# Bias additions in two halves, an ordered A^T, one warming matmul fewer and outputs sent by ScalarE, in a four-layer graph kernel on one core

## The chip, the cores and the metric

The kernel runs on one core of a Trainium2 chip, in one launch. The metric is the device time in microseconds (us); the median of several runs counts. The engines have short names in the profile: PE is TensorE (PEld its weight loads), DVE is VectorE, ACT is ScalarE, POOL is GpSimd and SP is SyncE, which here only issues DMAs.

## The reference

64 graphs share one adjacency A of 256 nodes, with 128 features for each node. Four layers follow each other; each adds its result to its input and normalises over the features. Cut to what matters:

```python
def reference(x, adj, ...):            # x [64, 256, 128], adj [256, 256], float32
    # layer 0: Chebyshev stack A x, A^2 x, A^3 x, with both adjacencies the same one
    x = layernorm(x + sum_k (A^k x) W_k)
    # layer 1
    x = layernorm(x + A (x W) + bias)
    # layer 2: A_norm = D^-1/2 (A + I) D^-1/2
    x = layernorm(x + (A_norm x) W^T + b)
    # layer 3: five steps of a gated unit, input h = x
    for step in range(5):
        m = A h                         # in_matrix and out_matrix are both A
        av = concat(m, m)
        u3 = h @ u3_w.T + u3_b
        z = sigmoid(av @ w3_w.T + w3_b + u3)
        r = sigmoid(av @ w4_w.T + w4_b + u3)
        hv = tanh(av @ w5_w.T + w5_b + (r * h @ u5_w.T + u5_b))
        h = (1 - z) * h + z * hv
    return layernorm(x + h)
```

## The kernel before

The 64 graphs are cut into 32 groups of two. A group's features fill one tile of 128 partitions by 512 (two graphs, two halves of the nodes, 128 features), and its whole path through the four layers is recorded as a list of operations. A group is named by its first graph: 0, 2, 4 and so on to 62.

The order of the instructions is not written by hand. Every operation is put into a planner with an engine, a cost, a lag until its result counts as there, a rank (mostly the group's number) and its inputs and outputs. `Plan.order` makes twelve attempts at a list schedule. The first has the bare ranks; in the others each rank has a small random addition. The attempt with the shortest planned end gives the order in which all instructions are issued, each engine's queue in that order. Any changed operation can therefore change the order everywhere. The planner's costs and lags are fixed numbers in the code: an SP load of x, for example, has a lag of its own for each of the first four groups, whatever else is on its way. Up to twelve groups are in flight, each some stages behind the one before.

Matrix products with A run in two forms. For the first three groups and at the start they are plain. For the others a product with a 2x2 block matrix is done in seven block products instead of eight (`seven` and `inner_seven`): GpSimd builds differences of the inputs (ts at L806 and L810, tq at L813), TensorE multiplies in an opening, one block more, and the rest; ScalarE saves the first block before it is added to (us, usq, usg at L848) and VectorE puts the blocks together (m, mq, mg at L832 to L842). "pm", "pmq", "pmg" are the PSUM banks of such products. In layer 0 VectorE also forms sums of two SBUF tiles (sd L690, ss L693, se L696, sf L699).

Normalisation in layers 0 to 2 is `spread_of` and `normalise_centred`: ScalarE squares and accumulates (L551), GpSimd takes the power −1/2 (rs, L555), ScalarE scales (L612). In layers 1 and 2 GpSimd adds the bias to the layer's input (yb, L977, in `record`), and VectorE adds this to the product of TensorE (s, L619). For 28 groups the state of layer 3 goes out to DRAM and comes back in another layout (dn, hn) before VectorE adds the residual (s, L624).

At the start, TensorE does seven warming matmuls on zeros. Then it transposes A (`turned_early`, banks p_at0 and p_at1), ScalarE and VectorE copy one half each to aT (`halved`, L298 and L299), TensorE squares A (`square`, p_a), and the two halves of A^2 transposed are copied in the same way. Between these stand the transposes ptx of the first loads of x. float32 matmuls stand in the trace as two passes.

At the end, the last two groups, 60 and 62, use `ended`. Their outputs lie in two PSUM banks of 256 columns; ScalarE squares the first half (L575), VectorE takes the statistics of the second (L580 to L584), GpSimd the power (L595). Then ScalarE scales a quarter (L599), VectorE the other half and after it the quarter that is left (L590), and SP sends the two halves (L604).

The DMAs of the kernel are nearly all issued from SP, in the order of its queue; GpSimd issues eight small loads of biases.

Of the kernel before, what the change touches and what calls it, by code (L numbers as in the profile page):

```python
# [12 lines left out]
OP = mybir.AluOpType  # L13
AX = mybir.AxisListType

P = 128
# [6 lines left out]
FINE = 8  # L23
END = 8
STEPS = 5
WARM = 7
ONES = (0, 0)
EPS = 1e-5
BANKS = 8
# [151 lines left out]
def kernel(  # L181
# [30 lines left out]
    nc = tc.nc  # L212
# [25 lines left out]
    def pre(rank, engine, cost, run, reads=(), writes=(), lag=None, joint=False, after=()):  # L238
        lag = lag or {"SP": 2300, "PE": 260, "DVE": 260, "ACT": 130, "POOL": 100}[engine]
        return plan.add(engine, cost, lag, rank, run, reads, writes, after, joint)  # L240
# [55 lines left out]
    def halved(v, ps):  # L296

        pre(-8, "ACT", act_cost(N), lambda: nc.scalar.copy(v.ap[:, 0, :], ps[0].ap[:, :N]), [ps[0]], [v], joint=True)  # L298
        pre(-8, "DVE", 420, lambda: nc.vector.tensor_copy(v.ap[:, 1, :], ps[1].ap[:, :N]), [ps[1]], [v], joint=True)  # L299

    for mt in range(T):
        pre(-8, "PE", 440, lambda mt=mt: turned_early(mt), [a_nat], [p_at[mt]])
    halved(aT, p_at)
    for mt in range(T):
        pre(-8, "PE", 870, lambda mt=mt: square(mt), [a_nat, aT], [p_a2[mt]])
    halved(a2T, p_a2)


# [162 lines left out]
    class Group:  # L471
# [90 lines left out]
        def ended(self, s):  # L562


            y, st, mv, ve, rs = (self.val(k, n + "3") for k, n in (
                ("w", "y"), ("st", "st"), ("mv", "mv"), ("ve", "ve"), ("rs", "rs")))
            halves = [range(t * self.q // 2, (t + 1) * self.q // 2) for t in range(2)]

            def place(q):
                t, i = divmod(q, self.q // 2)  # L570
                return s[t].ap[:, i * P:(i + 1) * P]

            def squares():
                for q in halves[0]:
                    nc.scalar.activation(nat(y)[:, q, :], place(q), AF.Square, scale=C ** -0.5,  # L575
                                         bias=root[:, 0:1], accum_out=ve.ap[:, q:q + 1])

            def stats():
                for q in halves[1]:
                    nc.vector.bn_stats(st.ap[:, q * 6:(q + 1) * 6], place(q))  # L580
                for q in halves[1]:
                    nc.vector.bn_aggr(mv.ap[:, 2 * q:2 * q + 2], st.ap[:, q * 6:(q + 1) * 6])
                q = halves[1]
                nc.vector.tensor_scalar(ve.ap[:, q.start:q.stop], mv.ap.rearrange("p (q k) -> p k q", k=2)[:, 1, q.start:q.stop],  # L584
                                        EPS, None, op0=OP.add)

            def scaled(t, first):
                q, n = halves[t], self.q // 2
                lo = q.start + first
                nc.vector.tensor_tensor(nat(y)[:, lo:q.stop, :], s[t].ap[:, first * P:n * P].rearrange("p (q c) -> p q c", c=C),  # L590
                                        rs.ap[:, lo:q.stop, None].to_broadcast([P, n - first, C]), op=OP.mult)

            self.act(squares, [s[0]], [y, ve], 390 * self.q // 2, True)
            self.dve(stats, [s[1]], [st, mv, ve], 260 * self.q // 2 + 110, True)
            self.add("POOL", 1040, 100, lambda: nc.gpsimd.tensor_tensor(rs.ap, ve.ap, half[:, :self.q], op=OP.pow),  # L595
                     [ve], [rs])
            h0, h1 = Val("const", [P, 1], "y0"), Val("const", [P, 1], "y1")
            h0.tile = h1.tile = root
            self.act(lambda: nc.scalar.mul(nat(y)[:, 0, :], place(0), rs.ap[:, 0:1]), [s[0], rs, y], [h0], 390)  # L599
            self.dve(lambda: scaled(1, 0), [s[1], rs, y], [h1], 380)  # L600
            self.dve(lambda: scaled(0, 1), [s[0], rs, y, h0], [h0], 230)
            for t, h in ((1, h1), (0, h0)):
                q = halves[t]
                self.add("SP", 450, 2400, lambda q=q: nc.sync.dma_start(self.view(out)[:, q.start:q.stop], nat(y)[:, q.start:q.stop]),  # L604
                         [y, h], [])

        def normalise_centred(self, tag, s):
            y, rs = self.spread_of(tag, s)
# [337 lines left out]
        def record(self):  # L946
# [26 lines left out]
            for tag, ats, w, bias in (("1", aT, w1c, b1c), ("2", anT, w2T, b2c)):  # L973
                yb = self.val("w", "yb" + tag)

                def biased(yb=yb, y=y, bias=bias):
                    nc.gpsimd.tensor_tensor(nat(yb), nat(y), bias[1][:, None, :].to_broadcast([P, self.q, C]),  # L977
                                            op=OP.add)

                self.add("POOL", 40 + 625 * self.nb, 100, biased, [y, bias[0]], [yb])  # L980
                m = self.propagate(tag, y, ats)
                py = self.val("bank", "py" + tag)

                def weight(py=py, m=m, w=w):
                    for q in range(self.q):
                        mm(py.ap[:, q * P:(q + 1) * P], m.ap[:, q * P:(q + 1) * P], w[1], True, True)

                self.pe(pe_cost(P, self.q), weight, [m, w[0]], [py])
                y = self.normalise_centred(tag, self.added(tag, py, yb))
# [107 lines left out]
```

## Time and profile before

| what | value |
|---|---|
| median of 3 runs | 1331.43 us (1331.15 to 1331.56) |
| the profiled execution's own time | 1330.67 us |
| its span in the trace | 1328.9 us, 23277 instructions |
| PE busy | 1319.2 us, 99% |
| DVE, ACT, POOL busy | 1038.5 us, 771.5 us, 630.7 us |
| L977 (bias additions), 64 of 128x512 | 82.8 us, 1294 ns each |
| L806 (differences of 128x256) | 730 to 742 ns each |

Busy times add up what each engine worked on, also where another engine sets the pace, so an engine with a high share is not always the one that is waited for. A line of a group has the line of code, the engine, the operation, output and inputs by name, shapes, a count, then the sum of busy time, the mean length in ns, and the idle time of the engine before it with what ended it. A line of the timeline has the start and the length in us first; neighbouring instructions of one kind are merged (xcount), and their length is that of the whole row. In a list of waits an engine and the tile that it works on stand first, then what it waited for, then the sum in us, how often, and the longest.

### The profile page before, as it was taken

What the parts mean: (1) busy time and instruction counts of PE and PEld (TensorE: products, weight loads), DVE (VectorE), ACT (ScalarE), POOL (GpSimd) and SP (SyncE); (2) the same over time, 40 slices, a digit from 0 to 9 for tenths busy, and PEclk for the clock granted to TensorE, in tenths of its full rate; (3) what the DMA queues carried; (4) which work ended last, traced back from release to release, by engine and by line L of the source; (5) the groups of instructions that cost most, each with busy time, mean ns of one, the idle gap of its engine ahead of it and who ended that gap; (6) DMA issues with size and microseconds to landing.
All of it is one profiled execution on the core that took longest, in us unless ns stands there. A gap on an engine that the chain in (4) does not pass through costs nothing.

```text
span 1328.9 us, 23277 instructions
## 1 busy us (share of the span) xinstructions
PE 1319.2 (99%) x6907; PEld 925.0 (70%) x6907; DVE 1038.5 (78%) x2574; ACT 771.5 (58%) x2360; POOL 630.7 (47%) x994
## 2 busy tenths in 40 slices
PE   9999999999999999999999999999999999999998
PEld 8987656657767866656677777676767876565555
DVE  7967777888797777778878777888877778777786
ACT  4777553545557765545465675655555688444445
POOL 4887531426176464415264573634434575222222
PEclk9999999999999999999999999999999999999999
DMA  7422343635234433545344333433441224444433
GB/s 186 122 59 63 90 107 82 154 95 133 73 87 112 112 88 89 127 108 139 95 115 109 88 96 96 106 93 104 104 104 56 66 63 142 98 108 92 95 80 95
DMA packets 402589, 133.87 MB, mean 101 GB/s; under 512 B 309760, under 2 KB 374400, under 8 KB 402464
## 3 DMA queue, kind: packets, MB, share of 16 engines
q1 hardware_dynamic: 402208, 132.26, 39.5%
q8 instruction: 55, 0.90, 0.3%
q0 software_dynamic: 256, 0.13, 0.2%
q14 instruction: 70, 0.57, 0.1%
HBM read 66.78 MB, written 65.27 MB: 99 GB/s over the span
## 4 chain that ended last, share of the span: by engine, by line
PE 99%; DVE 1%; issue 0%; ACT 0%; POOLq 0%; DVEq 0%; ACTq 0%
PE pr L222 31%; PE ph L222 21%; PE pmg L222 19%; PE py L222 12%; PE pm L222 7%; PE pz L222 4%; PE pmq L222 4%; PE s L222 1%; PE warm L222 0%; PE p_a L222 0%; DVE se L696 0%; DVE s L624 0%; PE ptx L863 0%; DVE sf L699 0%; POOLq L1092 0%
## 5 line engine op out<-in xcount | busy, mean ns | idle before, releaser
L222 PE MATMUL pr<-mg,w435u5T 128*128 128x512 f32 x640 | 321.0, 593 | 1.4 <-DVE mg L842 1.4
L806 POOL TENSOR_TENSOR tsg<-h 128x256 f32<-128x256 f32 x128 | 94.0, 734 | 306.4 <-DMA h<-dh 216.9
L912 ACT ACTIVATE r<-pr,bsum 128x512 f32<-128x512 f32 x160 | 105.5, 659 | 127.5 <-PE pr L222 111.3
L912 ACT ACTIVATE pr<-pr,bsum 128x512 f32<-128x512 f32 x160 | 105.4, 659 | 122.6 <-PE pr L222 122.0
L555 POOL TENSOR_TENSOR rs<-ve,half 128x4 f32<-128x4 f32 x98 | 100.5, 1026 | 147.6 <-ACT y L551 132.1
L943 DVE TENSOR_TENSOR d<-ph,hT 128x512 f32<-128x512 f32 x158 | 108.2, 685 | 71.5 <-ACT ph L912 67.3
L222 PE MATMUL ph<-rh,w435u5T 128*128 128x512 f32 x320 | 163.1, 593 | 0.0
L222 PE MATMUL pr<-hT,w2u3T 128*128 128x512 f32 x320 | 162.8, 593 | 0.0
L222 PE MATMUL ph<-mg,w435u5T 128*128 128x512 f32 x320 | 162.5, 593 | 0.0
L551 ACT ACTIVATE y<-s,root 128x128 f32<-128x128 f32 x392 | 152.8, 393 | 16.1 <-DVE s L619 13.5
L222 PEld LDWEIGHTS pr<-mg,w435u5T 128*128 128x128 f32 x640 | 109.0, 191 | 72.6 <-issue 57.4
L912 ACT ACTIVATE ph<-ph,bsum 128x512 f32<-128x512 f32 x158 | 104.0, 659 | 65.8 <-PE ph L222 65.1
L943 DVE TENSOR_TENSOR rh<-r,hT 128x512 f32<-128x512 f32 x160 | 109.1, 682 | 32.0 <-ACT r L912 30.7
L222 PEld LDWEIGHTS pmg<-aTp,h 128*128 128x128 f32 x512 | 88.0, 190 | 65.6 <-issue 43.0
L612 ACT ACTIVATE y<-s,rs 128x128 f32<-128x128 f32 x384 | 122.1, 393 | 4.5 <-POOL rs L555 4.1
L943 DVE TENSOR_TENSOR pr<-pr,d 128x512 f32<-128x512 f32 x156 | 107.6, 692 | 1.8 <-ACT pr L912 0.5
L943 DVE TENSOR_TENSOR hT<-hT,pr 128x512 f32<-128x512 f32 x156 | 105.7, 679 | 1.9
L222 PE MATMUL pmg<-s_aTp,tsg 128*128 128x128 f32 x768 | 106.7, 275 | 0.0
L222 PEld LDWEIGHTS ph<-rh,w435u5T 128*128 128x128 f32 x320 | 58.5, 190 | 63.5 <-issue 44.8
L977 POOL TENSOR_TENSOR yb<-y,wb 128x512 f32<-128x512 f32 x64 | 82.8, 1294 | 29.0 <-ACT y L612 28.9
L222 PE MATMUL pmg<-aTp,h 128*128 128x128 f32 x512 | 96.3, 274 | 0.0
L222 PEld LDWEIGHTS pmg<-s_aTp,tsg 128*128 128x128 f32 x768 | 96.0, 192 | 0.0
(212 smaller groups left out, 2782.2 us busy)
## 6 DMA issues: line engine op xcount, KB each, us to landing
dh<-th SPq DMA_DIRECT2D x160, 256.0 KB, 2.1
h<-dh SPq DMA_DIRECT2D x512, 64.0 KB, 2.4
x<-in_x_dram SPq DMA_DIRECT2D x32, 256.0 KB, 3.4
hT<-dh SPq DMA_DIRECT2D x128, 64.0 KB, 2.0
out_dram<-y SPq DMA_DIRECT2D x30, 256.0 KB, 2.4
dx<-tx SPq DMA_DIRECT2D x29, 256.0 KB, 2.6
xT<-dx SPq DMA_DIRECT2D x58, 128.0 KB, 2.6
dn<-tn SPq DMA_DIRECT2D x28, 256.0 KB, 2.0
```

Source lines behind the costliest of these rows:

```text
L222: nc.tensor.matmul(o, lhsT, rhs, start=start, stop=stop, skip_group_check=shared)
L551: nc.scalar.activation(nat(y)[:, q, :], nat(s)[:, q, :], AF.Square, scale=C ** -0.5, bias=root[:, 0:1], accum_out=ve.ap[:, q:q + 1])
L555: nc.gpsimd.tensor_tensor(rs.ap, ve.ap, half[:, :self.q], op=OP.pow)
L612: nc.scalar.mul(nat(y)[:, q, :], nat(s)[:, q, :], rs.ap[:, q:q + 1])
L806: nc.gpsimd.tensor_tensor(ts.ap[:, :2 * P].rearrange("p (x c) -> p x c", x=2), ins(h)[:, 1], ins(h)[:, :, 0], op=OP.subtract)
L912: self.act(lambda: nc.scalar.activation(t.ap, ps.ap, func, bias=bias[1], scale=1.0), [ps, bias[0]], [t], act_cost(self.width) + 100)
L943: self.dve(lambda: nc.vector.tensor_tensor(out(t), way(a), way(b), op=op), [a, b], [t])
L977: nc.gpsimd.tensor_tensor(nat(yb), nat(y), bias[1][:, None, :].to_broadcast([P, self.q, C]), op=OP.add)
```

## The change

- `WARM` is 6 instead of 7.
- The transposes and squares of A are chained in the plan, so that half 0 stands before half 1 on TensorE. Before, p_at1 came before p_at0.
- `ended`: ScalarE scales its whole half (`multiplied`), VectorE only the other (`scaled`). ScalarE's queue issues the DMA for its own half, SP's queue the other.
- Each bias addition on GpSimd becomes two instructions on 256 of the 512 columns. They are separate operations for the planner, with a cost of 735 each.

```diff
-WARM = 7
+WARM = 6
...
+    behind = ()
     for mt in range(T):
-        pre(-8, "PE", 440, lambda mt=mt: turned_early(mt), [a_nat], [p_at[mt]])
+        behind = (pre(-8, "PE", 440, lambda mt=mt: turned_early(mt), [a_nat], [p_at[mt]], after=behind),)
     halved(aT, p_at)
     for mt in range(T):
-        pre(-8, "PE", 870, lambda mt=mt: square(mt), [a_nat, aT], [p_a2[mt]])
+        behind = (pre(-8, "PE", 870, lambda mt=mt: square(mt), [a_nat, aT], [p_a2[mt]], after=behind),)
     halved(a2T, p_a2)
...
-            def scaled(t, first):
-                q, n = halves[t], self.q // 2
-                lo = q.start + first
-                nc.vector.tensor_tensor(nat(y)[:, lo:q.stop, :], s[t].ap[:, first * P:n * P].rearrange("p (q c) -> p q c", c=C),
-                                        rs.ap[:, lo:q.stop, None].to_broadcast([P, n - first, C]), op=OP.mult)
+            def multiplied():
+                for q in halves[0]:
+                    nc.scalar.mul(nat(y)[:, q, :], place(q), rs.ap[:, q:q + 1])
+
+            def scaled():
+                q = halves[1]
+                nc.vector.tensor_tensor(nat(y)[:, q.start:q.stop, :], s[1].ap[:, :len(q) * P].rearrange("p (q c) -> p q c", c=C),
+                                        rs.ap[:, q.start:q.stop, None].to_broadcast([P, len(q), C]), op=OP.mult)
...
-            self.act(lambda: nc.scalar.mul(nat(y)[:, 0, :], place(0), rs.ap[:, 0:1]), [s[0], rs, y], [h0], 390)
-            self.dve(lambda: scaled(1, 0), [s[1], rs, y], [h1], 380)
-            self.dve(lambda: scaled(0, 1), [s[0], rs, y, h0], [h0], 230)
-            for t, h in ((1, h1), (0, h0)):
-                q = halves[t]
-                self.add("SP", 450, 2400, lambda q=q: nc.sync.dma_start(self.view(out)[:, q.start:q.stop], nat(y)[:, q.start:q.stop]),
-                         [y, h], [])
+            self.act(multiplied, [s[0], rs, y], [h0], 770)
+            self.dve(scaled, [s[1], rs, y], [h1], 420)
+            for engine, e, q, h in (("SP", nc.sync, halves[1], h1), ("ACT", nc.scalar, halves[0], h0)):
+
+                def sent(e=e, q=q):
+                    e.dma_start(self.view(out)[:, q.start:q.stop], nat(y)[:, q.start:q.stop])
+
+                self.add(engine, 450, 2400, sent, [y, h], [])
...
-                def biased(yb=yb, y=y, bias=bias):
-                    nc.gpsimd.tensor_tensor(nat(yb), nat(y), bias[1][:, None, :].to_broadcast([P, self.q, C]),
-                                            op=OP.add)
-
-                self.add("POOL", 40 + 625 * self.nb, 100, biased, [y, bias[0]], [yb])
+
+                def biased(part, yb=yb, y=y, bias=bias):
+                    nc.gpsimd.tensor_tensor(nat(yb)[:, part], nat(y)[:, part],
+                                            bias[1][:, None, :].to_broadcast([P, self.q // 2, C]), op=OP.add)
+
+                for i in range(2):
+                    self.add("POOL", 735, 100, partial(biased, slice(i * self.q // 2, (i + 1) * self.q // 2)),
+                             [y, bias[0]], [yb], True)
```

In the changed program every engine's order differs from the first ten microseconds on. In SP's order the load of the raw weights of layer 0 (w_raw) stands between the first and the second load of x; before, it stood after the second.

## The prediction

> **What bounds the kernel now.** I read the page's busy shares and its chain first, then TensorE's own waits, then the timeline around each of the few places where TensorE stood.
>
> ```profile
> PE 1319.2 (99%) x6907; PEld 925.0 (70%) x6907; DVE 1038.5 (78%) x2574; ACT 771.5 (58%) x2360; POOL 630.7 (47%) x994
> PE 99%; DVE 1%; issue 0%; ACT 0%; POOLq 0%; DVEq 0%; ACTq 0%
> ```
>
> TensorE is busy for 1319.2 of 1328.9 us and carries 99% of the chain that ends last. Its records show first pass at 1.06 and last end at 1322.5. So any edit can act in three places only: before TensorE is fed (the first 13 us), where it waits, and after 1322.5. All else lies beside it.
>
> ```profile
> PE pr L222 <- DVE mg L842: 1.4, 1, 1.4
> PE warm L222 <- DVE root L263: 1.1, 1, 1.1
> PE pmq L222 <- DVE mq L838: 0.3, 1, 0.3
> ```
>
> These are nearly all the named waits of TensorE. A wait hides part of its price, because a matmul's record ends late. From pass start to pass start I find 0.7 us lost at 35.0 to 36.0, 2.5 at 377.9 to 385, and 0.5 in pieces elsewhere after 13 us. VectorE is named for both large ones; the timeline tells why it was late:
>
> ```profile
> 374.45 1.38 DVE L699 TENSOR_TENSOR sf<-mq,se 128x256 f32<-128x256 f32 x1
> 377.96 2.95 POOL L977 TENSOR_TENSOR yb<-y,wb 128x512 f32<-128x512 f32 x2
> 378.00 1.80 DVE L624 TENSOR_TENSOR s<-hn,y 128x512 f32<-128x512 f32 x1
> 379.72 1.48 DVE L696 TENSOR_TENSOR se<-ss,xT 128x256 f32<-128x256 f32 x1
> 381.13 0.74 DVE L842 TENSOR_TENSOR mg<-pmg,usg 128x256 f32<-128x256 f32 x2
> 381.59 1.12 PE L222 MATMUL pr<-mg,w435u5T 128*128 128x512 f32 x2 [1.42 <-DVE mg L842]
> ```
>
> L624 has a usual length of 0.68, L696 and L699 of 0.42. Here they take 1.80, 1.48 and 1.38, each beside a bias addition of L977; mg, which TensorE needs, is queued behind them. At 34.44 the same holds: L690 takes 1.32 beside an L977 that starts at 33.98, and mq of L838 comes late.
>
> **What the skill says.** "SBUF — State Buffer", section "SBUF: two separate sides": a VectorE instruction with two SBUF inputs and a GpSimd instruction that reads SBUF exclude each other, for the whole instruction. The trace agrees: the stretched ones all have two SBUF inputs, and s of L624 ends 0.4 after the first of the two yb. "DMA: Bandwidth & Descriptors", section "Queues, rings and completion order": each DMA engine takes descriptors in ring order, and SP and ACT have rings on the same 16 engines. The trace agrees for SP (below); no row has a DMA issued from ACT. "TensorE: Matmul & The Clock Gate", Part 1: the warm-up is some 3.4 us of time, not a number of matmuls. Here passes of 128 columns come every 0.213 us until 4.6, then every 0.11: 3.5 us after the first.
>
> **Part 1, the start.**
>
> ```profile
> 0.75 0.44 SPq L252 DMA_DIRECT2D a_nat<-in_adj_dram  x1
> 1.24 1.01 SPq L948 DMA_DIRECT2D x<-in_x_dram  x2
> 2.29 0.50 SPq L252 DMA_DIRECT2D w_raw<-in_L_gnn_weight_dram  x1
> 4.21 0.77 PE L290 MATMUL p_at<-ident,a_nat 128*128 128x128 f32 x4
> 5.44 1.99 PE L222 MATMUL p_a<-aT,a_nat 128*128 128x256 f32 x8
> 7.27 0.60 PE L863 MATMUL ptx<-ident,x 128*128 128x128 f32 x4
> ```
>
> a_nat lands 2.9 us after its issue, at 3.65, but p_at starts at 4.21, behind the warm passes. Six instead of seven take away two passes of 0.213: p_at can start at 3.79. It still runs at the slow clock until 4.6, where its four passes then end, with ptx to 5.04. With the halves in order, the first square needs only ScalarE's half, copied from p_at0: ready at about 4.83. So p_a starts at 5.04 instead of 5.44 and, without the slower first pass after a wait, ends at 6.77 instead of 7.27: 0.5 gained.
>
> But the plan is drawn anew, and the changed program's order has the load of w_raw before that of the second x; before, it stood after. Both are issued from SP, one issue each. A read of the two landings, median us in the last column:
>
> ```profile
> w_raw<-in_L_gnn_weight_dram SPq DMA_DIRECT2D x1, 448.0 KB, 6.1
> x<-in_x_dram SPq DMA_DIRECT2D x1, 256.0 KB, 4.9
> ```
>
> The second x (issued at 1.75) landed at 6.7, w_raw (2.29) at 8.4. Swapped in the same rings, x comes when all those bytes have passed: 8.4. The second ptx, next after the squares in both orders, waits for it, and everything of TensorE stands behind it. It starts at 8.45 instead of 7.27: **+1.2**. Bounds: x at 6.7 (no delay) gives −0.5; 8.7 gives +1.5. I take 8.4, as ring order has no reason to do better. The other moves on SP (weights in another order, aTp one place later, x of group 8 before that of 10) feed work from 13 us on; x of 8 lands about 15, its GpSimd reader has to 34.
>
> **Part 2, what follows to 40 us.** Counting TensorE passes on from 8.45 in the new order (0.216 for 256 columns, 0.11 for 128), the fifth block of pmq for group 12 is reached near 37.5. It needs ScalarE's copy usq_12. From the copy of v of group 4, whose data is ready at 25.1, there stand on ScalarE: three normalisations (1.28 each), two rows of squares (1.62), six copies of 256 (0.34), two more (0.58, 0.38) and eight of 128 (0.24), together 12.0, and about 1.1 of waits for TensorE: done at 38.2 to 38.5. So TensorE waits **+0.9**, and 0.2 at two narrower places. The unchanged order's loss at 35 (0.7) goes. Sum of the part +0.4; bounds −0.7 (ScalarE keeps up) and +1.5.
>
> **Part 3, the bias additions.** GpSimd adds 128x256 in 0.735 (row L806), so a pair costs 1.47 for 1.294:
>
> ```profile
> L977 POOL TENSOR_TENSOR yb<-y,wb 128x512 f32<-128x512 f32 x64 | 82.8, 1294 | 29.0 <-ACT y L612 28.9
> ```
>
> 64 × 0.176 = 11.3 us more on GpSimd, which is idle for half the span; the cover is narrowest at 50 to 100 us, where it is busy 43.1 of 50, and nine additions fall: 1.6 more, 44.7 of 50. If the cover went, ts of L806 would be late and TensorE with it. What VectorE can lose to one of them falls from 1.3 to 0.74. With each block halved, 2.2 us of lateness at 378 become some 1.2, of which TensorE's lead takes most. But the order is redrawn: other pairs meet, and 31 of the 64 pairs stand back to back. After 40 us the kernel before lost 2.9; I take 1.9 for the new one, my estimate: **−1.0**. Bounds −2.9 (nothing lost) and +4 (one late transfer, below).
>
> **Part 4, the end.**
>
> ```profile
> 1323.78 2.16 SPq L604 DMA_DIRECT2D out_dram<-y  x4
> 1324.60 0.37 ACT L599 ACTIVATE y<-s,rs 128x128 f32<-128x128 f32 x1 [1.23 <-POOL rs L595]
> 1324.60 0.69 DVE L590 TENSOR_TENSOR y<-s,rs 128x256 f32<-128x256 f32 x2 [0.65 <-POOL rs L595]
> ```
>
> Scales are ready at 1324.57. Before: VectorE's second product ends at 1325.29, SP's last issue starts at 1325.52, behind SP's other one, and lands 1.9 later. After: ScalarE scales two (L612 does four in 1.28, so 0.67) to 1325.27 and issues at about 1325.35: −0.17. The wait put into ScalarE's queue is for its own product; behind the first such issue (1323.7 to 1324.15) stands only the last group's scaling, which waits for 1324.57 anyhow. An issue from ACT isn't shown: bounds −0.4 and +0.4. VectorE loses two products of 0.27, beside these.
>
> **Sum.** +1.2 +0.4 −1.0 −0.2 = **+0.4 us**. The profiled execution took 1330.67 (span 1328.9 and 1.8 around it), so 1331.1; the median of runs stands 0.76 higher, 1331.43, so the forecast is **1331.8**. About 0.2%, 2.7 us, is what a measurement of this kernel can tell from no change.
>
> **The rivals.**
> - **Locks were the whole matter (faster).** The second x isn't late (−0.5), ScalarE keeps up, and halved blocks leave TensorE nothing to wait for: −0.5 −0.7 −2.5 −0.2 = −3.9, 1327.5. For it: both large losses lie beside L977. Against it: the ring order. Chance 0.12.
> - **A transfer comes late in the redrawn order (slower).** Place: SP's queue between 150 and 1000 us. At 360.7 to 368.2 twelve issues of h stood ahead of dn, whose source was done at 364.9; hn landed at 374.6, and L624 only came up at 378.0, so 3.4 us of lead were left. In an order that brings such a sum 4 us sooner, VectorE stands at it, and mg behind it. One such meeting costs up to 3.4; with the rest +0.4, 1335.2. It decides from 2.3 us of lateness. For it: nothing but the plan's assumed times guards these waits. Against it: the kernel before shows none. Chance 0.31.
> - **The start costs, the halving brings nothing back**: +1.2 +0.4 +0 −0.2 = +1.4, 1332.8, within the bound, together with the likeliest case 0.57.
>
> **Range.** 1328.0 to 1337.0: it reaches nearly to the faster case, and past the price of a late transfer by 1.8 for the bounds of the rest; the middle case's own range is 1328.8 to 1334.1. Faster by over 0.2%: 0.12; within: 0.57; slower: 0.31.
>
> **What would show it.** Right: second ptx starting at 8.3 to 8.6 with a wait on a DMA; p_a at 5.0; a wait on ScalarE's usq near 38; yb instructions of 0.74; no VectorE instruction stretched by more than 0.8 beside them; last landing 1.9 after an ACT issue near 1325.35 plus the shift. Wrong: ptx at 6.8, TensorE waits of over 2 us behind a DMA or behind GpSimd's ts, or a slow clock again after the stop at 7 us.

## The result, and the profile after

The changed kernel took **1332.48 us** (median of 22 runs, 1331.04 to 1338.18). The kernel before took 1331.12 beside it (22 runs, 1329.65 to 1332.14). The ratio is 1.0013, 95% interval 1.0007 to 1.0019: about 1.4 us slower, surely not faster, and within the 0.2% (2.7 us) that the prediction called no change. The forecast was 1331.8 in a range of 1328.0 to 1337.0.

The profiled execution of the changed kernel took 1333.69, which is 1.2 above its median; that of before lay 0.45 below its own. So the two spans differ by more (1331.8 − 1328.9 = 2.9 us) than the medians (1.4). I sum the trace against the spans and judge the size of an effect by the medians.

The page after, busy shares and the chain that ended last:

```profile
PE 1320.4 (99%) x6905; PEld 925.4 (69%) x6905; DVE 1035.8 (78%) x2572; ACT 770.5 (58%) x2362; POOL 643.4 (48%) x1058
PE 93%; DVE 3%; DMA 2%; ACT 1%; issue 0%; SPq 0%; POOLq 0%; DVEq 0%; ACTq 0%
```

TensorE still sets the end, but 6% of the chain now runs through VectorE, DMAs and ScalarE, where before it was 1%. GpSimd has 12.7 us more, and no wait of TensorE names it. TensorE's waits after, without the 1.1 us at the very start that both kernels have (waited for, sum in us, times, longest):

```profile
PE ptx L868 <- DMA x<-in_x_dram: 0.9, 1, 0.9
PE pm L222 <- ACT us L853: 0.8, 2, 0.4
PE ph L222 <- DVE rh L948: 0.7, 1, 0.7
PE pm L222 <- DVE m L843: 0.6, 1, 0.6
PE py L222 <- DVE v L724: 0.5, 1, 0.5
PE pz L222 <- DVE v L724: 0.3, 1, 0.3
PE pmq L222 <- ACT usq L853: 0.2, 1, 0.2
```

The reader is to see an exchange. The wait for mg of 1.4 us at 381 and that for mq at 35 are gone; seven smaller ones at other places stand instead, and only the first was forecast with its place and size. The loss of TensorE is counted from the start of one pass to the start of the next, as what exceeds the median for the shape (0.112 us for 128 columns, 0.216 for 256, 0.429 for 512). So counted, it lost 5.5 us before and 8.9 after. Of the 3.4 us more, 1.9 lie in the first 50 us and 1.5 behind them: 1.6 at 55 to 66 us, 0.9 at 278, 0.3 at 696, 1.0 at 803 and 0.7 at 1094, less the 2.5 that went at 378 to 385 and 0.5 in smaller pieces. The span grew by 2.9 only, as one warming matmul less saves 0.2 and the tail behind the last pass is 0.27 shorter.

TensorE's timeline at the start, after:

```profile
3.82 1.09 PE L290 MATMUL p_at<-ident,a_nat 128*128 128x128 f32 x4
4.70 0.87 PE L868 MATMUL ptx<-ident,x 128*128 128x128 f32 x4
5.41 1.89 PE L222 MATMUL p_a<-aT,a_nat 128*128 128x256 f32 x8
8.23 0.66 PE L868 MATMUL ptx<-ident,x 128*128 128x128 f32 x4 [0.93 <-DMA x<-in_x_dram]
```

p_at starts 0.39 sooner, as the one warming matmul less allows. But p_a starts at 5.41, as good as before (5.44), because the slow clock lasted until 5.1 here and until 4.4 before (the end of the last pass at the slow pace). The second ptx waits for its x, which landed at 8.19, behind w_raw at 7.30.

The group of the bias additions:

```profile
L983 POOL TENSOR_TENSOR yb<-y,wb 128x256 f32<-128x256 f32 x128 | 94.4, 748 | 30.0 <-ACT y L617 30.0
```

A half takes 748 ns. Over all VectorE instructions that started while a bias addition ran and took at least 0.15 us longer than the median of their kind, the excess fell from 8.4 us (longest 1.12) to 4.4 us (longest 0.52), each time over ten instructions.

### The profile page after: what moved, and what is told of

It is laid out like the page before. It is cut to its first block, busy times and chain, and to the rows that moved or that the text cites. A ratio compares the mean times of both kernels' runs of the same rounds, so it can differ in the third digit from the quotient of the medians.

```text
span 1331.8 us, 23325 instructions
## 1 busy us (share of the span) xinstructions
PE 1320.4 (99%) x6905; PEld 925.4 (69%) x6905; DVE 1035.8 (78%) x2572; ACT 770.5 (58%) x2362; POOL 643.4 (48%) x1058
## 4 chain that ended last, share of the span: by engine, by line
PE 93%; DVE 3%; DMA 2%; ACT 1%; issue 0%; SPq 0%; POOLq 0%; DVEq 0%; ACTq 0%
PE pr L222 30%; PE ph L222 20%; PE pmg L222 18%; PE py L222 10%; PE pm L222 7%; PE pz L222 3%; PE pmq L222 3%; DMA xT<-dx 1%; DMA x<-in_x_dram 1%; DVE tx L962 1%; PE s L222 1%; DMA dx<-tx 0%; ACT y L552 0%; DVE sd L695 0%; DMA dh<-th 0%
## 5 line engine op out<-in xcount | busy, mean ns | idle before, releaser
L983 POOL TENSOR_TENSOR yb<-y,wb 128x256 f32<-128x256 f32 x128 | 94.4, 748 | 30.0 <-ACT y L617 30.0
```

Of the source, the lines that this page charges most:

```text
L983: nc.gpsimd.tensor_tensor(nat(yb)[:, part], nat(y)[:, part], bias[1][:, None, :].to_broadcast([P, self.q // 2, C]), op=OP.add)
```

## The experiments

**Theory.** The change's own edits are together a gain, because the halved additions take away what TensorE loses beside them. What makes the kernel slower is that other operations in the plan give another order everywhere: the x behind w_raw at the start, and new meetings of instructions later. **Rival 1:** the edits themselves cost, or bring nothing. **Rival 2:** orders are worth the same, so the order is not the cause.

In "kernel before in its own order", an edit is made inside the function that an operation issues, so that costs, operations and random numbers of the planner stay and every engine keeps its queue. A single load is moved in the finished list. All runs, in three sessions, each with the kernel before beside them on the same chip:

| run | median us (range, n) | before in the same session | ratio, 95% interval |
|---|---|---|---|
| e1_warm6 | 1330.76 (1328.42 to 1333.33, 13) | 1330.79 | 1.0000, 0.9992 to 1.0008 |
| e2_halves | 1329.21 (1328.66 to 1331.84, 13) | 1330.79 | 0.9992, 0.9984 to 1.0000 |
| e3_w_first | 1331.62 (1329.66 to 1332.53, 13) | 1330.79 | 1.0007, 0.9999 to 1.0015 |
| e4_end | 1330.59 (1328.80 to 1331.41, 13) | 1330.79 | 0.9998, 0.9989 to 1.0006 |
| e5_x_first | 1332.26 (1330.05 to 1339.16, 13) | 1330.97 | 1.0015, 1.0004 to 1.0027 |
| e6_whole | 1334.94 (1332.80 to 1336.76, 5) | 1330.97 | 1.0033, 1.0021 to 1.0046 |
| e7_draw2 | 1330.31 (1329.39 to 1330.92, 13) | 1330.97 | 0.9994, 0.9986 to 1.0002 |
| e7_draw3 | 1335.83 (1333.18 to 1337.96, 5) | 1330.97 | 1.0039, 1.0025 to 1.0052 |
| e8_x_early | 1333.18 (1331.23 to 1338.09, 10) | 1330.66 | 1.0027, 1.0015 to 1.0039 |
| e9_all | 1329.03 (1327.93 to 1334.38, 14) | 1330.66 | 0.9998, 0.9988 to 1.0007 |
| e10_all_draw2 | 1329.68 (1329.27 to 1330.78, 13) | 1330.66 | 0.9991, 0.9983 to 0.9999 |
| e11_x_late | 1332.72 (one run) | 1330.66 | none |

### One warming matmul less

```diff
-WARM = 7
+WARM = 6
```

> The kernel before with six warming matmuls instead of seven, everything else and the whole order as it was. Theory (the slow clock ends a fixed time after TensorE's first pass, so leaving out 0.43 us of warming lets p_at start at 3.8 instead of 4.2 and p_a at about 5.2): second ptx at 6.8 to 7.0 instead of 7.27, kernel 0.2 to 0.4 us faster, 1330.8. Rival (the slow clock lasts longer when there is less warming, as the profile of the changed kernel with p_a at 5.41 and the clock slow until about 5.25 suggests): p_at at 3.8, but p_a again at 5.4 and second ptx at 7.2 to 7.3, time unchanged within 0.2 us.

The time is the same. In the profile p_at stands at 3.78, p_a at 5.30 and the second ptx at 7.14, in the middle between theory and rival. The slow clock ended at 4.6 here. It can't be told from one profile whether the 0.13 us come from the edit: over the fourteen profiles of this study the slow clock ended anywhere between 4.3 and 7.2 us, with seven warming matmuls (4.4, 4.6, 5.1, 5.5, 5.7, 5.9, 6.8) as with six (4.3, 4.6, 5.1, 5.9, 6.8, 7.15, 7.16). That spread is far larger than the two passes of 0.213 us.

### The halved additions alone, in the old order

```diff
-                    nc.gpsimd.tensor_tensor(nat(yb), nat(y), bias[1][:, None, :].to_broadcast([P, self.q, C]),
-                                            op=OP.add)
+                    for q in (slice(0, self.q // 2), slice(self.q // 2, self.q)):
+                        nc.gpsimd.tensor_tensor(nat(yb)[:, q], nat(y)[:, q],
+                                                bias[1][:, None, :].to_broadcast([P, self.q // 2, C]), op=OP.add)
```

> The kernel before in its own order on every engine, with each bias addition issued as two GpSimd instructions of 256 columns, one behind the other. Theory (halving lowers VectorE's stretch, and the changed order hid the gain): VectorE's instructions beside yb are stretched by 0.75 us at most, their sum beside yb falls from 8.4 to about 4.5 us; the TensorE wait for mg at 381.6 (1.4 named, 2.5 lost in all at 378 to 385) shrinks to 0.5 or less and the one at 35 stays or shrinks; kernel 1.0 to 2.5 us faster, 1328.6 to 1330.1. Rival (the halving itself costs: GpSimd is later by 0.18 us a pair, its two halves take VectorE's turn twice): the loss at 378 to 385 stays over 2 us or new waits come at 50 to 100 us, kernel the same or up to 1.5 us slower.

1.6 us faster by the medians, with an interval that ends at no change. The place is the one forecast. The timeline of this run around 378 us:

```profile
377.29 3.44 POOL L978 TENSOR_TENSOR yb<-y,wb 128x256 f32<-128x256 f32 x4
377.31 1.26 DVE L624 TENSOR_TENSOR s<-hn,y 128x512 f32<-128x512 f32 x1
378.50 0.95 DVE L696 TENSOR_TENSOR se<-ss,xT 128x256 f32<-128x256 f32 x1
379.38 0.74 DVE L842 TENSOR_TENSOR mg<-pmg,usg 128x256 f32<-128x256 f32 x2
379.84 0.30 PEld L222 LDWEIGHTS pr<-mg,w435u5T 128*128 128x128 f32 x2 [0.34 <-DVE mg L842]
379.84 1.13 PE L222 MATMUL pr<-mg,w435u5T 128*128 128x512 f32 x2
```

L624 and L696 take 1.26 and 0.95 where they took 1.80 and 1.48 beside the whole additions, TensorE's matmul has no named wait for mg any more (1.42 before; only the weight load ahead of it, PEld, stood idle 0.34), and what it loses ahead of that pass is 0.11 instead of 1.6. Not all came as forecast: VectorE's excess fell to 5.5 us (longest 0.58) and not to 4.5, and the 0.6 that TensorE loses some 3 us later (at 383.1, before at 384.9) stayed. The slow clock lasted until 5.9 in this profile and the second ptx stands at 7.76, 0.5 later than in the profile of before, and still the span is 1.2 shorter. That halving costs, the one half of rival 1, is refuted. That it brings nothing isn't excluded by the interval alone; against it speaks the loss at 380 that is gone here, and gone again in e9_all below.

### w_raw ahead of the second x, in the old order

```diff
+        ops = plan.order()
+        names = [op.vals[0].name if op.engine == "SP" else "" for op in ops]
+        moved = ops.pop(names.index("w0_raw"))
+        names.remove("w0_raw")
+        ops.insert(names.index("x_2"), moved)
```

> The kernel before with a single move: the load of w_raw stands on SP directly ahead of the second load of x instead of directly behind it. Theory (the transfers share the rings in order of issue): the second x lands at 8.1 to 8.5 instead of 6.7, second ptx starts at 8.2 to 8.5 instead of 7.27, kernel 0.9 to 1.2 us slower, 1332.0 to 1332.3. Rival (what TensorE loses at the start is made up by its shorter waits later, for instance at 35): second ptx late by the same 1 us but the time within 0.3 us of the kernel before.

TensorE's timeline of this run:

```profile
5.53 2.00 PE L222 MATMUL p_a<-aT,a_nat 128*128 128x256 f32 x8
9.14 0.66 PE L863 MATMUL ptx<-ident,x 128*128 128x128 f32 x4 [1.62 <-DMA x<-in_x_dram]
```

0.8 us slower, nearly as the theory had it, and with an interval that just includes no change. The transfer is later than expected: w_raw landed at 8.38 and x at 9.10, so the second ptx is 1.9 late. But the loss ahead of the pr that waits for mg near 381 shrank from 1.6 to 0.8. A late TensorE found its input nearer to ready: part of what the delay cost at the start came back at this wait.

### The end alone, in the old order

```diff
-            self.act(lambda: nc.scalar.mul(nat(y)[:, 0, :], place(0), rs.ap[:, 0:1]), [s[0], rs, y], [h0], 390)
+            self.act(lambda: [nc.scalar.mul(nat(y)[:, q, :], place(q), rs.ap[:, q:q + 1]) for q in halves[0]], [s[0], rs, y], [h0], 390)
...
-            self.dve(lambda: scaled(0, 1), [s[0], rs, y, h0], [h0], 230)
-            for t, h in ((1, h1), (0, h0)):
+            self.dve(lambda: None, [s[0], rs, y, h0], [h0], 230)
+            for t, h, e in ((1, h1, nc.sync), (0, h0, nc.scalar)):
```

> The kernel before in its own order, with the end of the changed kernel alone: ScalarE scales both of its quarters and issues the output of its half, VectorE's product of one quarter is left out. Theory: from the last power of GpSimd to the end of the span 4.05 to 4.15 us instead of 4.34, kernel 0.2 to 0.3 us faster, 1330.9. Rival (an issue from ScalarE costs as much as it saves): no less than 4.3 us from that power to the end, time unchanged.

```profile
1324.55 0.63 ACT L599 ACTIVATE y<-s,rs 128x128 f32<-128x128 f32 x2 [0.96 <-POOL rs L595]
1325.21 0.38 ACTq L604 DMA_DIRECT2D out_dram<-y  x1
```

From the last power to the end it is 4.07 instead of 4.34, as the theory said; the time is 0.2 lower, which can't be told from none. Yet the reading is not as plain as that. The issue from ScalarE stands 0.26 sooner after the power (0.69 instead of 0.95), but lands 2.10 after it instead of 1.90, so the last bytes are there only 0.07 us sooner. And the span's end falls in steps: 4.10 after the power in both other draws below and 4.64 in e2_halves, which have the old end, and 4.37 in e9_all, which has the new one. The 0.27 is therefore not shown to be the edit's. Nor is it shown that the issuing engine makes the 0.2: in this run ScalarE's issue stands 0.2 behind SP's (before, SP's two stood 0.46 apart), and in the pair before it, where SP's issue stands 0.11 behind ScalarE's, it is SP's that landed 2.07 after it. Two transfers so close to each other may be the reason.

### The second x first again, in the new order

```diff
+        ops = plan.order()
...
+        moved = ops.pop(names.index("x_2"))
+        names.remove("x_2")
+        ops.insert(names.index("w0_raw"), moved)
```

> The changed kernel with a single move: the second load of x stands on SP directly ahead of the load of w_raw, as before the change. Theory (0.8 to 1.1 us of the changed kernel's loss is this transfer): second ptx at 7.1 to 7.5 instead of 8.23, no wait on a DMA named for TensorE, kernel 0.6 to 1.0 us faster than the changed one (1332.5), so 1330.8 to 1331.5 beside 1330.8 to 1331.1 for the kernel before. Rival (the start is made up for elsewhere): ptx early, but the waits at 36 to 38 grow by as much, time 1332.2 or more.

This one falsified my expectation. The second ptx stands at 6.80, 1.4 us sooner than in the changed kernel, but the time is 1332.26 (some of its runs reach 1334 to 1339) and not near 1331. One wait of TensorE and the rows of VectorE that explain it:

```profile
PE pmq L222 <- DVE mq L843: 1.7, 1, 1.7
```

```profile
31.60 1.11 DVE L962 STREAM_TRANSPOSE tx<-x 128x512 f32<-128x512 f32 x1 [1.03 <-DMA x<-in_x_dram]
32.91 1.12 DVE L962 STREAM_TRANSPOSE tx<-x 128x512 f32<-128x512 f32 x1 [0.20 <-DMA x<-in_x_dram]
33.94 0.27 DVE L837 TENSOR_TENSOR usq<-usq,pmq 128x128 f32<-128x128 f32 x1
34.24 0.29 DVE L840 TENSOR_TENSOR wsq<-usq,pmq 128x128 f32<-128x128 f32 x1
34.44 0.82 DVE L695 TENSOR_TENSOR sd<-xT 128x256 f32<-128x256 f32 x1
35.19 0.27 DVE L843 TENSOR_TENSOR mq<-wsq,pmq 128x128 f32<-128x128 f32 x1
```

The mq that TensorE needs at 33.5 is ready at 35.5, because two transposes of later groups' x stand ahead of it in VectorE's queue, and their loads landed at 31.58 and 32.89. In the changed kernel these landed at 31.45 and 32.77: TensorE's better start doesn't bring them forward. TensorE loses 2.0 us there, where the changed kernel loses 1.4 at 37.0 to 38.4; up to 50 us, 1.1 of the 1.5 won before 13 us are lost again. Behind 50 us this one profile loses 0.9 less than that of the changed kernel, and its span is 1.3 shorter; but by the medians, each against the kernel before in its session, the two differ by 0.1 only (+1.3 and +1.4). The start costs and gains of the prediction are thus no addends in this order.

### Whole additions again, in the new order

```diff
-                    nc.gpsimd.tensor_tensor(nat(yb)[:, part], nat(y)[:, part],
-                                            bias[1][:, None, :].to_broadcast([P, self.q // 2, C]), op=OP.add)
+                    if part.start == 0:
+                        nc.gpsimd.tensor_tensor(nat(yb), nat(y), bias[1][:, None, :].to_broadcast([P, self.q, C]),
+                                                op=OP.add)
```

> The changed kernel in its own order on every engine, but each bias addition is one instruction of 512 columns again, issued where the first of the two halves stood. Theory (halving is a gain in this order too, as it was in the order of the kernel before, where it brought 1.0 to 1.6): VectorE's stretch beside yb rises from 4.4 to 7 us or more, TensorE loses 0.5 to 2 us more after 40 us, kernel 1333 to 1334.5. Rival (no yb meets an instruction that TensorE waits for in this order): VectorE is stretched more, but TensorE loses nothing more; 1332.2 to 1332.7.

The median of five runs is 2.5 us above that of the changed kernel, but the forecast reasons are there only in part. VectorE's excess beside the additions is 4.5 us (seven instructions, longest 1.10), no more than with halves and not 7 or more. At one place, though, what was expected happens. VectorE beside whole additions, in this run:

```profile
81.84 1.52 DVE L704 TENSOR_TENSOR sf<-mq,se 128x256 f32<-128x256 f32 x1
84.62 1.50 DVE L701 TENSOR_TENSOR se<-ss,xT 128x256 f32<-128x256 f32 x1
```

and the same two instructions in the changed kernel, where a half runs as sf starts and none beside se:

```profile
79.13 0.42 DVE L704 TENSOR_TENSOR sf<-mq,se 128x256 f32<-128x256 f32 x1
81.14 0.41 DVE L701 TENSOR_TENSOR se<-ss,xT 128x256 f32<-128x256 f32 x1
```

Behind them TensorE lost 1.7 us at 85.0 (a wait of 1.58 for ScalarE's us), where the changed kernel loses 0.1. That this execution was late by then isn't the reason. The run e8_x_early below has halves and was later still. The same two instructions took the usual time there, and TensorE lost 0.1 at that pass:

```profile
83.59 0.42 DVE L704 TENSOR_TENSOR sf<-mq,se 128x256 f32<-128x256 f32 x1
85.80 0.42 DVE L701 TENSOR_TENSOR se<-ss,xT 128x256 f32<-128x256 f32 x1
```

So in the new order too the halves are worth some 1.7 us at one place. In sum they aren't: behind 50 us TensorE lost 4.2 us with whole additions, 4.1 in the changed kernel and 3.8 in e8_x_early, as the loss of 1.0 at 803 is not there with whole ones. What sets this profile apart lies before 50 us (7.8 lost instead of 4.8), and is no effect of the edit: the first addition stands at 27 us, and by then VectorE was some 3 us later than in the changed kernel already. Its slow clock lasted until 7.2:

```profile
5.48 2.71 PE L222 MATMUL p_a<-aT,a_nat 128*128 128x256 f32 x8
```

p_a takes 2.71 instead of 1.89, A^2 comes late to VectorE, and VectorE's rows of 10 to 22 us meet GpSimd at other moments and are stretched (three additions for w0s take 1.47 instead of 0.99, the copy to ahat 0.94 instead of 0.42). Its x loads come late in turn, and TensorE stands for 3.2 us at 34.7. This profile is of the latest of the five runs (1336.76, with a mean granted clock of 0.997). The other four, 1332.8 to 1335.8, had 0.999 and have no trace, so where they lose stays open, and with it how much the halves bring in this order: 2.5 us by the medians, 0.1 by the traces behind 50 us.

### Two other draws of the order

```diff
-        best, rng = None, random.Random(1)
+        best, rng = None, random.Random(2)
```

> The kernel before, nothing changed but the seed of the planner's random additions (2 for 1): another order of the same instructions. Theory (a redraw alone moves the time by as much as the whole change did): it differs from the kernel before by more than 0.5 us either way, with other places of TensorE's waits after 13 us, their sum between 1.5 and 8 us (3.2 before). Rival (orders with equal planned length are equal on the chip, so the loss of the changed kernel comes from its own edits): within 0.4 us of the kernel before.

> The same with seed 3. Theory: again another sum of TensorE's waits, 1.5 to 8 us after 13 us, and a time that differs by more than 0.5 us from the kernel before or from seed 2. Rival: within 0.4 us of both.

The instructions are those of the kernel before, and the times are 0.7 below it (with an interval that just includes no change) and 4.9 above it. So a redraw alone can move the time by more than the whole change did, and by seed 3 rival 2 falls. Behind 50 us TensorE lost 0.1 us with seed 2 and 6.3 with seed 3, where it was 2.6 in the kernel before and 4.1 in the changed one (after 13 us 2.3 and 8.6, the second above the expected 1.5 to 8). Seed 3 loses nearly all at one place; TensorE, VectorE and GpSimd there:

```profile
112.05 0.77 PE L222 MATMUL pmq<-s_a2T,x 128*128 128x128 f32 x2 [3.17 <-DVE mq L838]
113.03 1.91 PE L222 MATMUL py<-w2u3T,m 128*128 128x128 f32 x8
```

```profile
105.42 5.75 DVE L693 TENSOR_TENSOR ss<-xT,mq 128x256 f32<-128x256 f32 x1
111.09 0.27 DVE L835 TENSOR_TENSOR wsq<-usq,pmq 128x128 f32<-128x128 f32 x1
```

```profile
105.38 1.27 POOL L977 TENSOR_TENSOR yb<-y,wb 128x512 f32<-128x512 f32 x1
...
110.44 0.45 POOL L810 TENSOR_TENSOR tsq<-x,tsq 128x128 f32<-128x128 f32 x1
```

An instruction of 0.42 us on VectorE (its median in the kernel before) took 5.75: it came free only 0.3 after the last of eleven GpSimd instructions without a gap between them. That these held it up is read from their standing side by side. mq and TensorE stood behind it for 3.3 us, and then the slow clock took TensorE until 118 (eight passes of 128 columns in 1.91 us).

### Two loads of x moved up in the new order

```diff
+        for name in ("x_16", "x_18"):
+            names = [op.vals[0].name if op.engine == "SP" else "" for op in ops]
+            moved = ops.pop(names.index(name))
+            sent = [i for i, op in enumerate(ops) if op.engine == "SP" and op.vals[-1].name == "xT_8"]
+            ops.insert(sent[0], moved)
```

> The changed kernel with the second x ahead of w_raw (as in the run e5_x_first), and in addition the loads of x for groups 16 and 18 moved up on SP, from between the dx transfers to directly ahead of the xT transfers of group 8. Theory (the 1 us won at the start was lost again because VectorE's transposes tx of those two loads, ahead of mq in VectorE's queue, waited for their landing at 31.6 and 32.9): they land at 28 or earlier, tx no longer waits there, the loss of TensorE at 33.5 falls from 1.9 to under 1 us, kernel 0.8 to 1.5 us faster than e5_x_first's 1332.3. Rival (the rings are full until 37 us, so moving a load up delays xT and dx by as much): the wait moves to another row of VectorE, loss and time as in e5_x_first within 0.4 us.

No gain: 1333.18, so the theory's repair failed; with 0.9 more than e5_x_first it is also outside the 0.4 of the rival. In the profiled execution, which was a late one (1338.09), the two loads landed at 30.6 and 31.6, not by 28, and their transposes no longer waited. The wait moved on to xT, as the rival said:

```profile
32.86 0.43 DVE L695 TENSOR_TENSOR sd<-xT 128x256 f32<-128x256 f32 x1 [1.41 <-DMA xT<-dx]
```

It had the long slow clock too (until 7.15), the same late and stretched VectorE rows as e6_whole, and a stop of TensorE for 3.6 us beyond its usual pace:

```profile
33.94 0.83 PE L222 MATMUL pmq<-s_a2T,tsq 128*128 128x128 f32 x6
...
38.47 0.80 PE L222 MATMUL pmq<-s_a2T,x 128*128 128x128 f32 x2 [3.47 <-DVE mq L843]
...
40.34 1.49 PE L222 MATMUL pmq<-s_a2T,tsq 128*128 128x128 f32 x6
```

Six passes of one kind take 0.83 before the stop and 1.49 after it; the full clock is back at 44.6. From e6_whole and this run together I read that this order turns a p_a that ends 0.9 us late (8.2 instead of 7.3) into a stop of over 3 us near 34.7, and pays for it twice: with the stop and with the slow clock behind it. Whether this also sets the late runs of the changed kernel (up to 1338.18) and of e5_x_first (1334 to 1339) apart stays open, as they have no trace. Each run's mean granted clock gives a hint: the two latest of e5_x_first and the three latest of e8_x_early have 0.996 or 0.997, all their others 0.998 to 1.0. The two latest of the changed kernel have 0.998, like two of its usual ones, so there it decides nothing.

### The change's edits without the new order

The two edits of e2_halves and e4_end and `WARM = 6`, with p_at0 ahead of p_at1:

```diff
+        ops = plan.order()
+        at = [next(i for i, op in enumerate(ops) if op.engine == "PE" and v in op.vals) for v in p_at]
+        ops[min(at)], ops[max(at)] = ops[at[0]], ops[at[1]]
```

> The kernel before in its own order, with all that the change does by itself: six warming matmuls, half 0 of A transposed ahead of half 1, each bias addition in two instructions back to back, ScalarE scaling and issuing its half at the end. Theory (the changed kernel's own edits are a gain of about 1.6, and only the new order costs): 1329.0 to 1329.7, that is 1.2 to 2 us faster than the kernel before. Rival (the edits get in each other's way also without a new order): 1330.5 or more.

> The same edits as in e9_all in the order that seed 2 gave (run e7_draw2, 1330.3, where VectorE's stretch beside bias additions was 3.3 instead of 8.4 us and TensorE had no loss beside one). Theory (the halving is worth what TensorE loses beside bias additions in the order at hand): nothing to gain from the halving here, 0.2 to 0.5 from the rest, 1329.8 to 1330.1. Rival (the halving is worth the same 1.3 us in any order): 1328.5 to 1329.2.

The theory holds for the median: 1329.03, 1.6 below the kernel before, and so 3.0 below the changed one, which lay 1.4 above it. Ten of its fourteen runs lie at 1327.9 to 1329.4, where only five of the 31 runs of the kernel before in that session do. Four lie at 1331.8 to 1334.4, and with these in it the ratio shows no gain; why they are late isn't known. In the profiles TensorE lost 0.7 us after 13 us here and 5.7 in the changed kernel, with the same edits: the order is what differs. In its profile the whole list of TensorE's waits is one line, the wait at the very start:

```profile
PE warm L222 <- DVE root L263: 1.1, 1, 1.1
```

The same edits in seed 2's order gave 1329.68, 0.6 below that order without them (1330.31, in another session) and between the two expectations. Half of the 0.6 is the session's, as the kernel before was 0.3 faster there too; the two spans differ by 0.04. This is the steadiest version with a median below both kernels (1329.27 to 1330.78; 0.9991 of the kernel before, with an interval that ends at 0.9999). The halves were worth 1.6 us where an addition had stood in TensorE's way; where none had, all the edits together brought 0.3 to 0.6.

### A later x, to see the clock

```diff
+        moved = ops.pop(names.index("x_2"))
+        names.remove("x_2")
+        ops.insert(names.index("x_6") + 6, moved)
```

> The kernel before with the second load of x moved further back on SP: behind w_raw, two more loads of x, wb and two raw weights. TensorE then stands still from about 7.2 us to 10.8, for 3.6 us or more. Theory (a stop of over 3 us throws TensorE back to the slow clock, as the rows after 34.7 in e6_whole and after 108.3 in e7_draw3 suggest): passes of 256 columns every 0.427 us and of 128 every 0.213 for 3 us or more after the stop, so that it costs 1.5 us or more beyond itself. Rival (the slow rows in those two runs had another cause, such as the shapes): passes at 0.216 and 0.11 at once after the stop, as after the stop of 1.8 us in e3_w_first.

Inconclusive. x landed at 10.14 and, the slow clock having kept p_a until 8.2, TensorE stood for only 2.0 us. The full clock came back at once, as after the 1.8 us of e3_w_first. So stops of 1.8 to 2.0 us left the clock alone, and stops of 3.2, 3.3 and 3.6 us (e6_whole, e7_draw3, e8_x_early) were each followed by 3 to 6 us of slow passes; the point between wasn't found. In the traces' record of the granted clock it falls to half at 37.9, 111.0 and 37.8, which is 2.3 to 3.0 us after the stop began, and comes back 3.4, 6.8 and 6.8 us later.

## Why the prediction was right, and where it was not

It was right in the time and in calling it no change of over 0.2%: +0.4 us forecast, +1.4 measured by the medians. Its own steps did less well than their sum. With a range 9 us wide, the time was hard to miss, and that it fell 0.7 from the forecast is in part luck. By the profiles, where the terms can be told apart, the span grew by 2.9: Part 1 brought 1.0, Part 2 0.4, Part 3 1.8 instead of −1.0, and Part 4 −0.3.

- **Part 1, the start, +1.2.** The mechanism held: x behind w_raw, TensorE waiting for it by name, +0.96 at the second ptx (8.23, forecast 8.45). The term for p_a (5.04) failed: 5.41. It took the slow clock's end at 4.6 from one profile as if it were a property of the kernel. With the slow clock over at 4.3 (e5_x_first, which has the same start but for the two loads) p_a did start at 5.08, so the rest of that term was sound. The Trainium skill, page "TensorE: Matmul & The Clock Gate", Part 1, says that the window is free-running and that the transition therefore depends on its phase at the start; I had used that section for the length only. The fourteen profiles agree that the end moves, but by more than the half microsecond either way that this part of the page gives: it came at 4.3 to 7.2 us. Priced in time, the step is +0.8 in the old order (e3_w_first) and nothing that could be told in the new one (e5_x_first), as the later wait for mq swallows it.
- **Part 2, to 40 us, +0.4.** The sum held: 1.1 us lost at 36.6 to 38.2 where the old order lost 0.7. The parts did not: ScalarE's usq costs 0.4 instead of 0.9, VectorE's m 0.8 instead of 0.2. Nor did the mechanism. ScalarE was not behind with its own work, as "together 12.0" has it; ahead of that usq it stood idle for VectorE, and VectorE for a transfer that landed at 35.69. The sum is right by luck:

```profile
35.78 0.55 DVE L695 TENSOR_TENSOR sd<-xT 128x256 f32<-128x256 f32 x1 [0.84 <-DMA xT<-dx]
36.56 0.27 ACT L858 COPY m<-pm 128x128 f32<-128x128 f32 x1 [0.81 <-DVE us L837]
36.72 0.27 ACT L853 COPY usq<-pmq 128x128 f32<-128x128 f32 x1
```

- **Part 3, the halves, −1.0.** This is the step that failed, with the wrong sign: +1.8. In the old order the effect of the halves was sized well (2.2 us of lateness "become some 1.2, of which TensorE's lead takes most"; e2_halves shows −1.6 in time). What failed is "I take 1.9 for the new one", the losses of a redrawn order after 40 us. They were 4.4 (before 2.6, by the same count; the prediction had 2.9): among them 0.6 at 55.6 behind two transposes of 1.11, 0.7 at 66.4 behind ScalarE's squares, 0.9 at 277.9 behind a transfer, 1.0 at 803 and 0.7 at 1094 behind ScalarE's scaling and squares. Halves have a share in two of them. In the unbroken row of VectorE ahead of 55.6, sf at 49.51 and sd at 50.34 start beside halves and take 0.49 and 0.52 longer than usual. At 803 sf takes 0.52 longer beside a half, and the rows around it are stretched by some 0.2 each beside GpSimd's differences:

```profile
801.92 1.54 DVE L704 TENSOR_TENSOR sf<-mq,se 128x256 f32<-128x256 f32 x2
803.39 0.67 DVE L695 TENSOR_TENSOR sd<-xT 128x256 f32<-128x256 f32 x1
804.72 1.12 PE L222 MATMUL ph<-rh,w435u5T 128*128 128x512 f32 x2 [0.73 <-DVE rh L948]
```

  In the chains of work ahead of the other three, 2.3 us in sum, no instruction is stretched beside a bias addition, so the halving doesn't touch them. The estimate scaled the old order's losses; seeds 2 and 3 show that another order has losses of its own (0.1 and 6.3 us behind 50 us). Two readings beneath it need a correction: s of L624 ended 0.55 after the first yb (379.80 and 379.25), not 0.4, and that the stretched ones all have two SBUF inputs holds beside the additions of the kernel before only. Of the ten in the changed kernel, four are a TENSOR_SCALAR of 128x4 with one input (ve, L534).
- **Part 4, the end, −0.17.** The span's end fell by 0.28, but the landing only by 0.07, as the issue from ScalarE took 0.2 us longer to land than the one from SP before.
- **The rivals.** "Locks were the whole matter" is refuted for the changed kernel and half right for the old order, where the halves alone bring 1.6 of its 2.5. "A transfer comes late" did happen between 150 and 1000 us:

```profile
277.53 0.63 DVE L695 TENSOR_TENSOR sd<-xT 128x256 f32<-128x256 f32 x1 [3.10 <-DMA xT<-dx]
```

  VectorE stood 3.1 us for a transfer and v behind it came late, but TensorE's lead left only 0.9 of it, under the point of 2.3 us from which that rival was to decide. "The start costs, the halving brings nothing back" (+1.4) has the right number, and for this order it isn't refuted: by the traces of e6_whole and of the changed kernel, the halves won 1.7 us at one place and hardly anything in sum, and the medians (2.5 us) leave it open. What it lacks is the losses that came with the order.
- **What would show it.** It came true that TensorE waits on the DMA (at 8.23, a little before 8.3 to 8.6), that halves take 0.75, and that no VectorE instruction is stretched by over 0.8 beside them; a wait on usq is there, but of 0.2. It did not come true that p_a starts at 5.0 and that the landing is 1.9 after ScalarE's issue (2.1).

In short, by medians: the edits in the old order −1.6 (e9_all, with an interval that doesn't exclude no change), the new order +3.0 on top, and +1.4 in all.

## What to carry to other kernels

Where a scheduler with random draws decides the order, an edit that adds or drops an operation changes two things, and the second can be the larger: measure the edit once inside the old order, and try a few draws before judging it. Short instructions on an engine that excludes another are worth what the excluded one's customer is late for, which the named waits show and the sum of stretched time (8.4 us here for 1.6 gained) does not. A gain ahead of a transfer that is not itself brought forward can be lost again at that transfer, as in e5_x_first.

## What I had not expected of the hardware

- A VectorE instruction with two SBUF inputs can be kept waiting by more than one GpSimd instruction. I had taken one as the limit. ss of L693 took 5.75 us instead of 0.42 across eleven of them in e7_draw3 (one such case in the fourteen profiles). "SBUF — State Buffer", section "SBUF: two separate sides", speaks of an exclusive lock for the whole instruction; how the next holder is chosen no run here shows, and beside the halves of the changed kernel no VectorE instruction lost more than 0.52.
- The slow clock at the start ended between 4.3 and 7.2 us with the same first pass at 1.06. It returned in the three stops of 3.2 us and more, 2.3 to 3.0 us after they began, and not in those of 1.8 to 2.0.
- A VectorE instruction with one SBUF input was stretched beside a bias addition as well: ve of L534 took 0.68 us instead of 0.17 at 1085.1 in the changed kernel.
- The last DMA landed 2.10 us after an issue from ScalarE and 1.90 after one from SP, with the transfer ahead of it 0.2 and 0.46 us before; which of the two differences counts isn't shown. The span's end behind it came in steps of about 0.3 us (4.05 to 4.10, 4.34 to 4.37, 4.64 after the last power).
